# Window attention and a Fourier layer on one Trainium2 core: transposing q and k on VectorE in 32-element blocks

## The chip, the cores and the metric

The kernel runs on one core of one Trainium2 chip. The metric is the device time of an execution in microseconds, the median over runs. TensorE (PE; PEld is its weight load), VectorE (DVE), ScalarE (ACT) and GpSimd (POOL) each work through a queue of their own, in order, and wait for each other through semaphores. SyncE (SP) issues the transfers.

## The reference

Two layers are applied to x of shape (8, 192, 64, 64), all in fp32. A token is a pixel with its 192 channels.

```python
# layer 0: attention in windows of 8 x 8 tokens, 6 heads of 32, then an MLP
shortcut = layer_norm(tokens(x), norm1_g, norm1_b)
q, k, v = windows(shortcut) @ qkv_w.T + qkv_b            # 64 tokens a window
attn = einsum('bhnd,bhmd->bhnm', l2n(q), l2n(k)) * temperature
kth = top_k(attn, 16)[..., -1:]
attn = where(attn >= kth, attn, -100.0)
attn = softmax(attn + rpb, axis=-1)
out = einsum('bhnm,bhmd->bhnd', attn, v) @ proj_w.T + proj_b
x2 = shortcut + out
x2 = x2 + gelu(layer_norm(x2) @ fc1_w.T + fc1_b) @ fc2_w.T + fc2_b
# layer 1: a pointwise network on the 2-D spectrum, then an MLP
xf = fft2(layer_norm(x2), norm='ortho')
h = gelu([xf.real, xf.imag] @ fc1_w.T + fc1_b) @ fc2_w.T + fc2_b     # 2 -> 16 -> 2
x3 = x2 + ifft2(h, norm='ortho').real
out = x3 + gelu(layer_norm(x3) @ mlp1_w.T + mlp1_b) @ mlp2_w.T + mlp2_b
```

## The kernel before

An image of 64 x 64 pixels is cut into eight bands of 512 tokens (eight windows). A band is done in the generators `front` (load, transpose to tokens, layer norm, back to channels, q, k and v, their norms), `attention` (once for each half band `hb`, four windows and six heads) and `back` (projection, MLP of layer 0). Layer 1 of an image follows in twelve groups of 16 channels, `forward`, `pointwise`, `inverse` (the transforms as products with cosine and sine matrices, and the network between them), and in eight bands of `leave` (MLP and store). `mlp` is shared by `back` and `leave`: for each of three pairs of 128 hidden units the products L587 (channels 0 to 127) and L600 (the other 64, in 64-row tiles), Gelu (L571), and at the end L630.

q, k and v of a band: `part_a` multiplies the first 128 channels of the normalized tokens `xn` by the weights, q and k into `pq` (L744) and v into `pv` (L745), with the same 128 tokens as stationary operand; `part_b` does the same for the other 64 channels in two 64-row tiles (L758) and adds the bias of q and k (L761). The index p is one half of the tokens each time, and a row of `pq` is a token. The results are copied to `qk` and `vv` through the helper `copy` (L786), squared and summed for the norms (L708 or L710, L712), and the norms' inverse roots are taken on GpSimd.

The attention of a half band: q and k are scaled by their norms (L798); eight TensorE transposes of 96 x 128 turn them to channels (L804) into one PSUM tile `qt`, which ScalarE or VectorE copies to `qkt` (L786); 24 products of 64 x 64 (four windows, six heads) give the scores (L821), three row groups of 32 channels each; the scores are copied to `s`, the 16 largest of a row are found on VectorE by max, match_replace and max for each of twelve groups (L844 to L846), the others masked (L849, L851), and the softmax follows on GpSimd, ScalarE and VectorE (L854 to L864). TensorE transposes the weights (L871) and multiplies with v (L896).

Nothing runs in the order of the source. Each generator yields operations `op(engine, weight, mode, get, put, after, done)`, and `issue` plays them as a list scheduler while the program is built: it keeps a clock for each engine, takes among the operations that can start soon the one with the earliest begin plus urgency, where the urgency is 300 times the due time of its task (`at_band`, `at_group` and the lists in `streams`), and lets an operation of engine `EITHER` go to ScalarE or VectorE, whichever would end first. `get` and `put` count the buffers: four PSUM tiles `ps` of two banks each, one `qkt`, one `qk`, one `xn`, five `att`, seven `h`. `mode` is the shape of TensorE's tiles; a change of it is priced at 20 units. What comes out is one fixed order for each engine; the waits at run time are those of the semaphores.

Of the kernel before, what the change touches and what calls it, by code (L numbers as in the profile page):

```python
# [8 lines left out]
FP = mybir.dt.float32  # L9
# [6 lines left out]
C = 192  # L16
CA = 128
HC = 96
HW = 64
BAND = 512  # L20
HALF = 256
ROW = 768
# [6 lines left out]
def op(engine, weight, mode=None, get="", put="", after=None, done=None, put_too=""):  # L29
    return engine, weight, mode, get.split(), (put + " " + put_too).split(), after, done  # L30


def issue(streams, units):
# [26 lines left out]
    def start(queue):  # L60
        if queue[0]:
            gen, place = queue[0].pop(0)
            task = {"gen": gen, "queue": queue, "urgency": 300 * place, "last": (None, 0)}
            queue[1] += 1
            task["order"] = (queue[1], len(live), place)
            live.append(task)
            advance(task, None)

    for tasks, width in streams:
        queue = [list(tasks), 0]  # L70
        for _ in range(width):
            start(queue)
    while live:
        best, ready = {}, {}
        for task in live:
            engines, weights, kind, get, put, after, done = task["op"]
# [8 lines left out]
            for name in set(get):  # L85
                n = get.count(name)
# [19 lines left out]
        for engine, found in ready.items():  # L106
            first = min(begin + cost for _, begin, cost, *_ in found) + 15
# [14 lines left out]
        engine, begin, change_cost, task, weight = choice  # L122
        _, _, kind, get, put, after, done = task["op"]
# [15 lines left out]
def kernel(  # L139
# [18 lines left out]
    nc = tc.nc  # L158
    B = x.shape[0]
    NB = HW * HW // BAND  # L160
# [7 lines left out]
    def psum(name):  # L168
        return psp.tile([128, 2, 512], FP, tag="ps", name=name)
# [381 lines left out]
    def mlp(src, nm, w1, fc1_bias, w2, then=None):  # L551
# [12 lines left out]
        copy(done, hn, pc[:, :ROW])  # L564
        hs = []

        def gelu(fp, ph):
            yield op("act", 138, "gelu", put="ps", done=("gelu", nm, fp))
            h = sb.tile([128, 2, BAND], FP, tag="h", name=f"h_{nm}_{fp}", bufs=H_BUFS)
            for k in range(2):  # L570
                nc.scalar.activation(  # L571
                    h[:, k].rearrange("p (t n) -> p t n", t=2),
                    ph[:, :, k * HALF : (k + 1) * HALF],
                    AF.Gelu,
                    bias=fc1_bias[:, 2 * fp + k : 2 * fp + k + 1],
                )
            hs.append(h)

        for fp in range(3):
# [30 lines left out]
            for n, (weight, kind, product) in enumerate(halves[::-1] if fp == 1 else halves):  # L610
                get = ("ps h h h" if fp == 0 else "ps") if n == 0 else ""
                after = None if fp == 0 and n == 0 else []
                yield op(
                    "pe", weight, kind, get=get, put="hn" if fp == 2 and n == 1 else "", after=after
                )
                if n == 0:
                    ph = psum(f"mh_{nm}_{fp}")
                product(n == 0)
            yield from gelu(fp, ph)
        last = [("gelu", nm, fp) for fp in range(3)]  # L620
        for half in range(2):
            if half == 0:
# [20 lines left out]
    def front(b, i):  # L643
# [91 lines left out]
        def values(whole):  # L735
            done = yield op(EITHER, (80, 96), put="ps", after=[whole], done=("vv", b, i))
            copy(done, vv.rearrange("p t a c -> p t (a c)"), pv[:, :, : 2 * C])

        for p in range(2):
            def part_a(first):  # L740
                for t in range(2):
                    tok = xn[:, (2 * t + p) * 128 : (2 * t + p + 1) * 128]
                    flags = dict(start=first, stop=not first, skip_group_check=True)
                    nc.tensor.matmul(pq[:, t, : 2 * C], tok, wqkv[0][:, : 2 * C], **flags)  # L744
                    nc.tensor.matmul(  # L745
                        pv[:, t, p * C : (p + 1) * C], tok, wqkv[0][:, 2 * C :], **flags
                    )

            def part_b(first):
                flags = dict(skip_group_check=True, stop=not first)  # L750
                for to, cols in (
                    (pq[:, :, : 2 * C], slice(0, 2 * C)),
                    (pv[:, :, p * C : (p + 1) * C], slice(2 * C, 3 * C)),
                ):
                    for t in range(2):
                        rows = slice(64 * t, 64 * t + 64)
                        tok = xn[rows, BAND + p * 128 : BAND + (p + 1) * 128]
                        nc.tensor.matmul(to[:, t], tok, wqkv[1][rows, cols], start=first, **flags)  # L758
                for t in range(2):
                    rows = slice(64 * t, 64 * t + 64)  # L760
                    nc.tensor.matmul(  # L761
                        pq[:, t, : 2 * C], ones3[rows], qb3[rows], start=False, **flags
                    )

            if p == 0:
                yield op("pe", 192, "full", get=f"ps ps {places[0]} {places[1]}", after=[normal, "qkv"])
                pq, pv = psum(f"pq_{nm}_{p}"), psum(f"pv_{nm}")
                part_a(True)
                yield op("pe", 112, "row64")
                part_b(False)  # L770
            else:
                yield op("pe", 112, "row64", get="ps", after=[])
                pq = psum(f"pq_{nm}_{p}")
                part_b(True)
                whole = yield op("pe", 192, "full", put="xn")
                part_a(False)
            yield squares(p, pq)
        yield values(whole)

        yield op("pool", 368, after=[normal, "rows"], done=("xt", b, i))  # L780
# [3 lines left out]
    def copy(done, to, of):  # L784

        (nc.scalar.copy if done[0] == "act" else nc.vector.tensor_copy)(to, of)  # L786
# [3 lines left out]
    def attention(b, i, hb):  # L790
# [5 lines left out]
        nf = nrm.rearrange("p a h -> p (a h)")  # L796
        scale = nc.gpsimd if scaled[0] == "pool" else nc.vector
        scale.tensor_tensor(qk3, qk3, nf.unsqueeze(2).to_broadcast([128, 24, 32]), ALU.mult)  # L798
        yield op("pe", 87, "full", get="ps qkt", put=held[b, i][0] if hb == 1 else "")
        pt = psum(f"qt_{nm}")  # L800
        for j in range(2):
            for c in range(2):
                for p in range(2):
                    nc.tensor.transpose(  # L804
                        pt[:HC, j, c * 256 + p * 128 : c * 256 + (p + 1) * 128],
                        qk[:, p, j * C + c * HC : j * C + (c + 1) * HC],
                        ident,
                    )
        done = yield op(EITHER, (100, 121), put="ps")
        qkt = sb.tile([HC, 2, 2, 256], FP, tag="qkt", name=f"qkt_{nm}", bufs=1)  # L810
        copy(done, qkt.rearrange("p j c t -> p j (c t)"), pt[:HC])

        yield op("pe", 58, "s", get="ps ps att", put="qkt")
        ps01, ps2 = psum(f"s_{nm}_0"), psum(f"s_{nm}_1")
        pss = [ps01[:, 0], ps01[:, 1], ps2[:, 0]]
        for wi in range(4):
            for c in range(2):
                for h3 in range(3):
                    rows = slice(32 * h3, 32 * h3 + 32)
                    tok = slice(wi * 64, wi * 64 + 64)  # L820
                    nc.tensor.matmul(  # L821
                        pss[h3][64 * c : 64 * c + 64, tok],
                        qkt[rows, 0, c, tok],
                        qkt[rows, 1, c, tok],
                        start=True,
                        stop=True,
                    )
        done = yield op(EITHER, (59, 69), put="ps")
        s = sb.tile([128, 3, 4, 64], FP, tag="att", name=f"s_{nm}", bufs=ATT_BUFS)
        copy(done, s[:, 0:2].rearrange("p h w k -> p h (w k)"), ps01[:, :, :256])  # L830
        done = yield op(EITHER, (39, 43), put="ps")
        copy(done, s[:, 2].rearrange("p w k -> p (w k)"), ps2[:, 0, :256])

        shape = [128, 3, 4, 64]
        row = lambda t: t.unsqueeze(3).to_broadcast(shape)
# [145 lines left out]
    def forward(b, n):  # L981
# [36 lines left out]
        for j in range(2):  # L1018
            for e in range(2):
                for c in range(4):  # L1020
# [142 lines left out]
    def leave(b, j):  # L1163
# [40 lines left out]
    bands = [(b, i) for b in range(B) for i in range(NB)]  # L1204
    at_band = lambda b, i, late: b + i / NB + late
    groups = [(b, n) for b in range(B) for n in range(NG)]
    at_group = lambda b, n: b + 1.17 + .685 * n / NG
    layer1 = (vec(N2G), vec(N2B))
    streams = [
        ([(setup_qkv(), -1)], 1),  # L1210
# [2 lines left out]
        ([(setup_mlp(0, lambda: (wfc1, wfc2), vec(G2), vec(B2), ["rows", (None, 3000)]), -0.5)], 1),  # L1213
        ([(setup_layer1(), 0.2)], 1),
        ([(setup_mlp(1, lambda: wmlp, *layer1, ["layer1", ("att", 0, 5, 1)]), 0.2)], 1),
        ([(front(b, i), at_band(b, i, -.135)) for b, i in bands], 2),
        ([(attention(b, i, hb), at_band(b, i, .015)) for b, i in bands for hb in range(2)], 4),
        ([(back(b, i), at_band(b, i, .28)) for b, i in bands], 2),
        ([(forward(b, n), at_group(b, n)) for b, n in groups], 1),
        ([(pointwise(b, n, k), at_group(b, n)) for b, n in groups for k in range(2)], 2),  # L1220
        ([(inverse(b, n), at_group(b, n)) for b, n in groups], 1),
        ([(leave(b, j), b + 1.81 + .435 * j / NB) for b, j in bands], 2),
    ]
    with tc.manual_schedule():
        issue(streams, units)
# [80 lines left out]
```

## Time and profile before

| | |
|---|---|
| median of 3 runs | 4932.9 us (4930.42 to 4936.1) |
| profiled execution, its own time | 4943.11 us |
| its span | 4941.3 us |
| granted TensorE clock, mean | 0.977 |
| TensorE busy | 4702.8 us |
| VectorE busy | 2797.7 us |
| ScalarE busy | 2744.7 us |
| GpSimd busy | 2381.0 us |
| HBM read and written | 29.29 and 25.17 MB |

The times of the parts come from the one profiled execution; the span reaches from its first instruction to its last. A line such as "L804 PE MATMUL qt<-ident,qk ... x1024 | 151.7, 297 | 60.7 <-..." is a group of instructions: line, engine, operation, tile written and tiles read, count, busy time in us, mean duration in ns, and the idle time of the engine just before them with what ended it. An fp32 product appears as two records, a transpose as one. TensorE's records overlap each other, so that the mean duration is longer than the distance from one start to the next, and the busy times of groups that follow each other share some time. The slices at the top of the prediction are 40 equal parts of the span in tenths.

### The profile page before, as it was taken

How to read it: one execution, taken by the hardware profiler on the slowest of the kernel's cores; microseconds unless marked ns; L12 is line 12 of the kernel's file. 1: busy time of each engine (PE TensorE's matmuls, PEld its weight loads, DVE VectorE, ACT ScalarE, POOL GpSimd, SP SyncE). 2: the span in 40 equal slices, each digit the busy share in tenths (PEclk: the TensorE clock that was granted, in tenths of full speed). 3: DMA queues.
4: the chain of work that ended last, by engine and by line, in shares of the span. 5: the costliest groups of instructions: out<-in, count | busy, mean ns of one | idle time of the engine just before them, and what ended most of it. 6: DMA issues, size and time to landing. Idle time of an engine off the chain costs nothing.

```text
span 4941.3 us, 147257 instructions
## 1 busy us (share of the span) xinstructions
PE 4702.8 (95%) x63818; PEld 3780.0 (76%) x63818; DVE 2797.7 (57%) x10326; ACT 2744.7 (56%) x3866; POOL 2381.0 (48%) x2208
## 2 busy tenths in 40 slices
PE   6888999999999999999999999999999999999989
PEld 4667777886778877888678877788777887778768
DVE  6778566456665466655665556645666546562112
ACT  3555666446655566555755566645666456653553
POOL 5677555346554455454653555545555445541100
PEclk7898999999999999999999999999999999999999
DMA  2000000000000000000000000000000000000000
GB/s 55 11 8 11 9 9 5 23 14 9 9 12 17 18 6 9 13 19 15 9 5 14 22 14 6 9 14 24 9 6 9 20 18 9 2 2 20 9 2 26
DMA packets 54112, 64.09 MB, mean 13 GB/s; under 512 B 17583, under 2 KB 36218, under 8 KB 53466
## 3 DMA queue, kind: packets, MB, share of 16 engines
q1 hardware_dynamic: 53454, 54.68, 3.8%
q8 instruction: 502, 8.22, 0.7%
q14 instruction: 144, 1.18, 0.1%
q10 hardware_dynamic: 12, 0.00, 0.0%
HBM read 29.29 MB, written 25.17 MB: 11 GB/s over the span
## 4 chain that ended last, share of the span: by engine, by line
PE 85%; ACT 5%; DVE 5%; POOL 3%; issue 2%; DMA 0%; SPq 0%; ACTq 0%; DVEq 0%; POOLq 0%
PE mo_d L630 10%; PE mo_b L630 9%; PE fh L1067 8%; PE mh_d L587 7%; PE fo L1094 7%; PE mh_b L587 7%; PE mh_d L600 4%; PE mh_b L600 4%; PE pq L744 3%; ACT fh L1050 3%; PE qt L804 2%; PE fa L997 2%; PE at L871 2%; PE fb L1115 2%; PE fy L1142 2%
## 5 line engine op out<-in xcount | busy, mean ns | idle before, releaser
L1050 ACT ACTIVATE fh<-fh,ab 128x1024 f32<-128x1024 f32 x768 | 815.1, 1112 | 163.9 <-PE fh L1067 160.2
L854 POOL TENSOR_TENSOR s<-s,top 128x768 f32<-128x768 f32 x128 | 193.8, 1514 | 917.5 <-DVE s L851 870.8
L730 POOL TENSOR_TENSOR nrm<-nrm,mhalf 128x24 f32<-128x24 f32 x128 | 551.9, 4311 | 10.7
L630 PE MATMUL mo_b<-wfc,h_b 128*128 128x192 f32 x3072 | 518.0, 327 | 0.0
L630 PE MATMUL mo_d<-wmlp,h_d 128*128 128x192 f32 x3072 | 512.3, 327 | 0.0
L630 PEld LDWEIGHTS mo_b<-wfc,h_b 128*128 128x128 f32 x3072 | 499.2, 190 | 10.3 <-issue 5.8
L630 PEld LDWEIGHTS mo_d<-wmlp,h_d 128*128 128x128 f32 x3072 | 498.6, 190 | 7.2 <-issue 4.6
L1067 PE MATMUL fh<-fz,w1p 32*128 32x248 f32 (+1 forms) x6144 | 467.6, 404 | 30.1 <-ACT fh L1050 23.3
L571 ACT ACTIVATE h_d<-mh_d,fcb 128x512 f32<-128x512 f32 x384 | 242.1, 684 | 436.0 <-PE mh_d L600 278.1
L1067 PEld LDWEIGHTS fh<-fz,w1p 32*128 32x128 f32 x6144 | 293.0, 185 | 149.5 <-issue 67.3
L844 DVE MAX8 top<-s 128x8 f32<-128x64 f32 x1536 | 320.9, 209 | 129.0 <-ACT s L786 127.9
L1094 PE MATMUL fo<-fh,w2p 128*32 128x264 f32 (+1 forms) x6144 | 387.2, 389 | 3.9 <-ACT fh L1050 2.3
L846 DVE MAX8 top<-s 128x8 f32<-128x64 f32 x1536 | 349.9, 228 | 53.4
L587 PE MATMUL mh_b<-hn_b,wfc_a 128*128 128x256 f32 x1536 | 377.0, 389 | 3.2 <-ACT hn_b L786 1.9
L587 PE MATMUL mh_d<-hn_d,wmlp_a 128*128 128x256 f32 x1536 | 370.7, 386 | 0.8 <-ACT hn_d L786 0.8
L864 POOL TENSOR_TENSOR s<-s,rsum 128x768 f32<-128x768 f32 x128 | 191.2, 1494 | 300.4 <-DVE top L844 144.5
L587 PEld LDWEIGHTS mh_b<-hn_b,wfc_a 128*128 128x128 f32 x1536 | 280.0, 191 | 67.7 <-issue 26.5
L587 PEld LDWEIGHTS mh_d<-hn_d,wmlp_a 128*128 128x128 f32 x1536 | 280.6, 190 | 55.3 <-issue 18.1
L845 DVE MATCH_REPLACE8 s<-top,s 128x64 f32<-128x64 f32 x1536 | 320.3, 209 | 0.1
L1094 PEld LDWEIGHTS fo<-fh,w2p 128*32 128x32 f32 x6144 | 185.6, 111 | 152.8 <-issue 33.4
L571 ACT ACTIVATE h_b<-mh_b,fcb 128x512 f32<-128x512 f32 x384 | 243.1, 686 | 97.3 <-PE mh_b L600 50.6
L1180 DVE TENSOR_TENSOR zt<-mo_d,xy 128x768 f32<-128x768 f32 x64 | 61.3, 957 | 377.2 <-PE mo_d L630 345.5
(220 smaller groups left out, 9311.2 us busy)
## 6 DMA issues: line engine op xcount, KB each, us to landing
xin<-in_x SPq DMA_DIRECT2D x64, 256.0 KB
out<-z SPq DMA_DIRECT2D x64, 256.0 KB
xin<-in_x SPq DMA_DIRECT2D x128, 64.0 KB
out<-z SPq DMA_DIRECT2D x128, 64.0 KB
wfc<-in_wfc SPq DMA_DIRECT2D x1, 576.0 KB
wmlp<-in_wmlp SPq DMA_DIRECT2D x1, 576.0 KB
wfc_a<-in_wfc SPq DMA_DIRECT2D x1, 384.0 KB
wfc_b<-in_wfc SPq DMA_DIRECT2D x2, 192.0 KB
```

The lines of the kernel that those rows point to most:

```text
L571: nc.scalar.activation(h[:, k].rearrange("p (t n) -> p t n", t=2), ph[:, :, k * HALF : (k + 1) * HALF], AF.Gelu, bias=fc1_bias[:, 2 * fp + ...
L587: nc.tensor.matmul(ph[:, t, k * HALF : (k + 1) * HALF], w1[0][:, f], hn[:, t * HALF : (t + 1) * HALF], start=(first and k == 0), stop=not ...
L600: nc.tensor.matmul(ph[:, t, k * HALF : (k + 1) * HALF], w1[1][rows, f], hn[rows, BAND:ROW], start=(first and k == 0), stop=not first, skip ...
L630: nc.tensor.matmul(acc[:, j, t * C : (t + 1) * C], hs[f // 2][:, f % 2, q * 128 : (q + 1) * 128], w2[:, f, ORDER[t]], start=(f == 0 and t ...
L730: nc.gpsimd.tensor_tensor(nf, nf, mhalf[:, :24], ALU.pow)
L844: nc.vector.max(first, of)
L845: nc.vector.match_replace(s2, first, of, -3.0e38)
L846: nc.vector.max(top[:, k // 4, k % 4, 8:16], s2)
L854: nc.gpsimd.tensor_tensor(s, s, top[:, :, :, 0:1].to_broadcast(shape), ALU.subtract)
L1050: nc.scalar.activation(hs[hf, k], ph, AF.Gelu, bias=ab[:, 0:1])
L1067: nc.tensor.matmul(phs[k // 2][:, k % 2, cols], w1p[i][rows, hf].rearrange("p h v -> p (h v)"), fz[rows, :] if rhs is None else zu[rows, : ...
L1094: nc.tensor.matmul(po[rows, :] if i == 0 else pou[rows, :, 1 : U - 1], w2p[i][:, hf].rearrange("p a v -> p (a v)"), hs[hf, k // 2][:, k % ...
```

## The change

q and k are turned by one VectorE instruction per half band in place of eight TensorE transposes and a copy. It transposes blocks of 32 x 32: 32 tokens of one parity of one window against the 32 channels of one head. For that the products of q and k take their tokens with a stride of two (`by_block`), so that half p holds the tokens of parity p, and the 32 partitions of a quadrant hold one window's; the blocks of the two parities are written interleaved, which restores the order of tokens in `qkt`. The scores then lie in four row groups, one for each window, and in two PSUM tiles with two windows each. v keeps dense tokens and gets products of its own after those of q and k.

Beside it, the planner is given other numbers: urgency 360 in place of 300 per unit of due time, other due times, the Gelu of a pair of hidden units yielded after the products of the next pair, and the two copies of `fz` as two operations. The prices of TensorE's new operations and of the transpose are in the diff.

```diff
-            task = {"gen": gen, "queue": queue, "urgency": 300 * place, "last": (None, 0)}
+            task = {"gen": gen, "queue": queue, "urgency": 360 * place, "last": (None, 0)}
...
-        def gelu(fp, ph):
-            yield op("act", 138, "gelu", put="ps", done=("gelu", nm, fp))
+        def gelu(fp, ph, last):
+            yield op("act", 138, "gelu", put="ps", after=[last], done=("gelu", nm, fp))
...
-            yield from gelu(fp, ph)
+            if fp > 0:
+                yield from gelu(fp - 1, *held_)
+            held_ = ph, last
+        yield from gelu(2, *held_)
...
+        def by_block(half, p):
+            return half.rearrange("c (n b) -> c b n", b=2)[:, p]
+
+        def qk_a(pq, p, first):
+            for t in range(2):
+                tok = by_block(xn[:, t * HALF : (t + 1) * HALF], p)
+                nc.tensor.matmul(
+                    pq[:, t, : 2 * C], tok, wqkv[0][:, : 2 * C],
+                    start=first, stop=not first, skip_group_check=True,
+                )
...
+        yield op("pe", 128, "full", get=f"ps {places[0]} {places[1]}", after=[normal, "qkv"])
+        pq = psum(f"pq_{nm}_0")
+        qk_a(pq, 0, True)
+        last = yield op("pe", 80, "row64")
+        qk_b(pq, 0, False)
+        yield squares(0, pq)
+        yield op("pe", 80, "row64", get="ps", after=[])
+        pq = psum(f"pq_{nm}_1")
+        qk_b(pq, 1, True)
+        yield op("pe", 128, "full")
+        qk_a(pq, 1, False)
+        yield squares(1, pq)
+        yield op("pe", 128, "full", get="ps", after=[])
+        pv = psum(f"pv_{nm}")
...
+        whole = yield op("pe", 64, "row64", put="xn")
...
-        yield op("pe", 87, "full", get="ps qkt", put=held[b, i][0] if hb == 1 else "")
-        pt = psum(f"qt_{nm}")
...
-                    nc.tensor.transpose(
-                        pt[:HC, j, c * 256 + p * 128 : c * 256 + (p + 1) * 128],
-                        qk[:, p, j * C + c * HC : j * C + (c + 1) * HC],
-                        ident,
-                    )
-        done = yield op(EITHER, (100, 121), put="ps")
-        qkt = sb.tile([HC, 2, 2, 256], FP, tag="qkt", name=f"qkt_{nm}", bufs=1)
-        copy(done, qkt.rearrange("p j c t -> p j (c t)"), pt[:HC])
+        yield op("dve", 90, get="qkt", put=held[b, i][0] if hb == 1 else "")
+        qkt = sb.tile([128, 12, 64], FP, tag="qkt", name=f"qkt_{nm}", bufs=1)
+        nc.vector.transpose(
+            qkt.rearrange("p h (k a) -> p a h k", a=2), qk.rearrange("p a (h d) -> p a h d", d=32)
+        )
...
-        yield op("pe", 58, "s", get="ps ps att", put="qkt")
+        yield op("pe", 55, "s", get="ps ps att", put="qkt")
+        pss = [psum(f"s_{nm}_{k}") for k in range(2)]
+        for h3 in range(3):
+            for c in range(2):
+                for wi in range(4):
+                    rows = slice(32 * wi, 32 * wi + 32)
                     nc.tensor.matmul(
+                        pss[wi // 2][64 * c : 64 * c + 64, wi % 2, h3 * 64 : (h3 + 1) * 64],
+                        qkt[rows, 3 * c + h3],
+                        qkt[rows, 6 + 3 * c + h3],
...
-        yield op("dve", 118, put="ps ps", done=("fz", b, n))
         for k in range(2):
+            yield op("dve", 43 + 33 * k, put="ps", done=("fz", b, n) if k else None)
...
-    at_group = lambda b, n: b + 1.17 + .685 * n / NG
+    at_group = lambda b, n: b + 1.055 + .755 * n / NG
...
-        ([(front(b, i), at_band(b, i, -.135)) for b, i in bands], 2),
-        ([(attention(b, i, hb), at_band(b, i, .015)) for b, i in bands for hb in range(2)], 4),
-        ([(back(b, i), at_band(b, i, .28)) for b, i in bands], 2),
+        ([(front(b, i), at_band(b, i, -.12)) for b, i in bands], 2),
+        ([(attention(b, i, hb), at_band(b, i, -.07)) for b, i in bands for hb in range(2)], 4),
+        ([(back(b, i), at_band(b, i, .2)) for b, i in bands], 2),
...
-        ([(leave(b, j), b + 1.81 + .435 * j / NB) for b, j in bands], 2),
+        ([(leave(b, j), b + 1.69 + .55 * j / NB) for b, j in bands], 2),
```

More of the change, by code (lines that the diff above doesn't have):

```diff
@@ L612, in mlp @@
                 after = None if fp == 0 and n == 0 else []
-                yield op(
+                last = yield op(
                     "pe", weight, kind, get=get, put="hn" if fp == 2 and n == 1 else "", after=after
@@ L737, in values @@
             copy(done, vv.rearrange("p t a c -> p t (a c)"), pv[:, :, : 2 * C])
-        for p in range(2):
[L740 to L746, printed above, removed]
-                    )
[L749 to L777, printed above, removed]
@@ new lines, in by_block @@
+        def by_block(half, p):
[4 more added lines that the diff above has]
+                nc.tensor.matmul(
+                    pq[:, t, : 2 * C],
+                    tok,
+                    wqkv[0][:, : 2 * C],
+                    start=first,
+                    stop=not first,
+                    skip_group_check=True,
+                )
@@ new lines, in qk_b @@
+        def qk_b(pq, p, first):
+            flags = dict(skip_group_check=True, stop=not first)
+            for t in range(2):
+                rows = slice(64 * t, 64 * t + 64)
+                tok = by_block(xn[rows, BAND:ROW], p)
+                nc.tensor.matmul(
+                    pq[:, t, : 2 * C], tok, wqkv[1][rows, : 2 * C], start=first, **flags
+                )
+            for t in range(2):
+                rows = slice(64 * t, 64 * t + 64)
+                nc.tensor.matmul(pq[:, t, : 2 * C], ones3[rows], qb3[rows], start=False, **flags)
@@ new lines, in front @@
+        pv = psum(f"pv_{nm}")
+        for p in range(2):
+            for t in range(2):
+                nc.tensor.matmul(
+                    pv[:, t, p * C : (p + 1) * C],
+                    xn[:, (2 * t + p) * 128 : (2 * t + p + 1) * 128],
+                    wqkv[0][:, 2 * C :],
+                    start=(p == 0),
+                    stop=False,
+                    skip_group_check=True,
+                )
+        whole = yield op("pe", 64, "row64", put="xn")
+        for p in range(2):
+            for t in range(2):
+                rows = slice(64 * t, 64 * t + 64)
+                nc.tensor.matmul(
+                    pv[:, t, p * C : (p + 1) * C],
+                    xn[rows, BAND + p * 128 : BAND + (p + 1) * 128],
+                    wqkv[1][rows, 2 * C :],
+                    start=False,
+                    stop=True,
+                    skip_group_check=True,
+                )
@@ L798, in attention @@
         scale.tensor_tensor(qk3, qk3, nf.unsqueeze(2).to_broadcast([128, 24, 32]), ALU.mult)
-        yield op("pe", 87, "full", get="ps qkt", put=held[b, i][0] if hb == 1 else "")
-        pt = psum(f"qt_{nm}")
-        for j in range(2):
-            for c in range(2):
-                for p in range(2):
-                    nc.tensor.transpose(
-                        pt[:HC, j, c * 256 + p * 128 : c * 256 + (p + 1) * 128],
-                        qk[:, p, j * C + c * HC : j * C + (c + 1) * HC],
-                        ident,
-                    )
-        done = yield op(EITHER, (100, 121), put="ps")
-        qkt = sb.tile([HC, 2, 2, 256], FP, tag="qkt", name=f"qkt_{nm}", bufs=1)
-        copy(done, qkt.rearrange("p j c t -> p j (c t)"), pt[:HC])
-        yield op("pe", 58, "s", get="ps ps att", put="qkt")
[L814 to L820, printed above, removed]
+        yield op("dve", 90, get="qkt", put=held[b, i][0] if hb == 1 else "")
+        qkt = sb.tile([128, 12, 64], FP, tag="qkt", name=f"qkt_{nm}", bufs=1)
+        nc.vector.transpose(
+            qkt.rearrange("p h (k a) -> p a h k", a=2), qk.rearrange("p a (h d) -> p a h d", d=32)
+        )
+        yield op("pe", 55, "s", get="ps ps att", put="qkt")
+        pss = [psum(f"s_{nm}_{k}") for k in range(2)]
+        for h3 in range(3):
+            for c in range(2):
+                for wi in range(4):
+                    rows = slice(32 * wi, 32 * wi + 32)
                     nc.tensor.matmul(
-                        pss[h3][64 * c : 64 * c + 64, tok],
-                        qkt[rows, 0, c, tok],
-                        qkt[rows, 1, c, tok],
+                        pss[wi // 2][64 * c : 64 * c + 64, wi % 2, h3 * 64 : (h3 + 1) * 64],
+                        qkt[rows, 3 * c + h3],
+                        qkt[rows, 6 + 3 * c + h3],
                         start=True,
@@ L827, in attention @@
                     )
-        done = yield op(EITHER, (59, 69), put="ps")
         s = sb.tile([128, 3, 4, 64], FP, tag="att", name=f"s_{nm}", bufs=ATT_BUFS)
-        copy(done, s[:, 0:2].rearrange("p h w k -> p h (w k)"), ps01[:, :, :256])
-        done = yield op(EITHER, (39, 43), put="ps")
-        copy(done, s[:, 2].rearrange("p w k -> p (w k)"), ps2[:, 0, :256])
+        for k in range(2):
+            done = yield op(EITHER, (49, 56), put="ps")
+            copy(
+                done,
+                s[:, :, 2 * k : 2 * k + 2].rearrange("p h w k -> p w h k"),
+                pss[k][:, :, :C].rearrange("p w (h k) -> p w h k", h=3),
+            )
         shape = [128, 3, 4, 64]
```

## The prediction

> **What bounds the kernel now.** I read the busy table and the slices first, then the chain, then the stretches, and only then the groups of the lines that change.
>
> ```profile
> PE 4702.8 (95%) x63818; PEld 3780.0 (76%) x63818; DVE 2797.7 (57%) x10326; ACT 2744.7 (56%) x3866; POOL 2381.0 (48%) x2208
> ...
> PE   6888999999999999999999999999999999999989
> ...
> PE 85%; ACT 5%; DVE 5%; POOL 3%; issue 2%; DMA 0%; SPq 0%; ACTq 0%; DVEq 0%; POOLq 0%
> ```
>
> TensorE is busy for 95% of the span, every other engine for less than 60%, and the chain that ended last runs on TensorE for 85% of the way. A busy TensorE can still be a waiting one, so the stretches matter more (columns: length, then busy time of PE, PEld, DVE, ACT, POOL):
>
> ```profile
> 800.00:1600.00 800.00, 779.18 (x10158) 633.33 (x10157) 470.22 (x1736) 451.17 (x640) 383.58 (x371) 0.99 0.05 13
> 1600.00:2400.00 800.00, 777.58 (x10814) 625.32 (x10812) 464.84 (x1709) 463.21 (x648) 412.61 (x376) 1.00 0.04 13
> 2400.00:3200.00 800.00, 776.40 (x11366) 617.80 (x11368) 479.35 (x1755) 472.54 (x646) 403.85 (x368) 0.99 0.04 11
> ```
>
> In the steady part TensorE has 21 to 24 us of idle in 800, some 3%. So a microsecond of TensorE work taken out there is nearly a microsecond of the span. The idle that is left is 4941.3 - 4702.8 = 238.5 us, of which about 85 lie in the first 400 us (TensorE busy 66.7, 69.3 and 178.8 us in 100, 100 and 200). What ends it is in the waits (who waited for whom, us, times, longest):
>
> ```profile
> PE qt L804 <- DVE qk L798: 28.0, 5, 12.1
> PE fh L1067 <- ACT fh L1050: 23.3, 26, 1.6
> PE qt L804 <- POOL qk L798: 21.2, 3, 14.0
> PE fz L1022 <- ACT fh L1050: 19.0, 24, 1.9
> PE s L821 <- ACT qkt L786: 14.4, 13, 2.4
> ```
>
> Two kinds: TensorE at the transposes of q and k, waiting for their scaling (few and long, nearly all in the first 400 us), and TensorE waiting for ScalarE's Gelu to give a PSUM slot back (many, short).
>
> The groups that change, and a stretch of TensorE's timeline (start, length of the merged group):
>
> ```profile
> L804 PE MATMUL qt<-ident,qk 128*96 128x128 f32 x1024 | 151.7, 297 | 60.7 <-DVE qk L798 28.0 <-POOL qk L798 21.2 <-ACT fh L1050 8.7
> L786 ACT COPY qkt<-qt 96x1024 f32<-96x1024 f32 x106 | 106.8, 1007 | 115.3 <-PE qt L804 114.8
> L786 DVE COPY qkt<-qt 96x1024 f32<-96x1024 f32 x22 | 26.4, 1199 | 28.0 <-PE qt L804 27.6
> L712 DVE TENSOR_REDUCE nrm<-sq 128x24 f32<-128x768 f32 x128 | 121.1, 946 | 173.4 <-ACT sq L708 143.3 <-POOL sq L710 29.0
> ```
> ```profile
> 2002.10 1.08 PE L804 MATMUL qt<-ident,qk 128*96 128x128 f32 x8
> 2003.02 0.33 PE L924 MATMUL pp<-wprojr,ot 128*128 128x192 f32 x1
> ...
> 2015.78 0.91 PE L744 MATMUL pq<-wqkv_a,xn 128*128 128x384 f32 x2
> 2016.53 0.49 PE L745 MATMUL pv<-wqkv_a,xn 128*128 128x192 f32 x2
> 2016.85 0.81 PE L744 MATMUL pq<-wqkv_a,xn 128*128 128x384 f32 x2
> 2017.50 0.49 PE L745 MATMUL pv<-wqkv_a,xn 128*128 128x192 f32 x2
> ```
>
> Neighbouring groups overlap, so the group's 151.7 us is not what the span gives back. What it gives back is start to start: 2003.02 - 2002.10 = 0.92 us for the eight transposes of one half band.
>
> [...] No run here shows that instruction; the nearest row that reads 768 elements, L712, takes 946 ns. [...] the first pair of L744, straight after 32-row tiles, takes 0.75 us start to start, the second 0.65, so 0.10 us at the entry. [...] no run here shows a strided weight load.
>
> **The change, part by part.**
>
> *Transposes off TensorE.* 64 bands x 2 halves = 128 times 0.92 us = 117.8 us less of TensorE. Bounds: 8 x 0.109 us (the spacing inside a group) x 128 = 112 below, the group's 151.7 above. I take 117.8, all on the path, for 97% of the steady stretch is TensorE's.
>
> *Evacuation of the transposes gone.* ScalarE loses 106.8 us, VectorE 26.4. Both had cover, so nothing directly; PSUM loses one tenant per half band.
>
> *Transposes on VectorE.* 128 times 0.95 us [...] = 121 us. With 26.4 gone and, by the order of the new program, fewer copies and normalizations there (98 tensor_scalar of about 0.45 us go to ScalarE), VectorE rises by about 50 to 95 us, to at most 2893 of some 4810 us, 60%. The cover is its 40% of idle, so zero; without cover it is 121 us. The wait it adds: the transpose stands in VectorE's queue behind whatever series of maxima or statistics is ahead, after the scaling and after the last scores that read `qkt` (one buffer). Behind it on VectorE wait the next half band's maxima. TensorE's s matmuls wait for it, and all that stands behind them in TensorE's queue. The old chain, 0.92 us transposes and a 1.0 us copy, is replaced by one step of 0.95, so the path from scaling to scores is 1 us shorter. Bounds: 10 us better (the startup waits at qt, 49 us, lose part) to 0.5 us worse at each of 128 (64 us). I take 0: the startup waits turn up at s.
>
> *Scores.* The same 24 products per half band, now in four row groups in place of three. The group's busy time, 108.6 us, is 0.85 us per half band. If the pace is that of the row groups it falls by a quarter (27 us), if it is that of issuing, by nothing. I take 8. Evacuation: 512 and 256 elements (585 and 381 ns on ScalarE) become twice 384, the same sum.
>
> *v by its own products.* Same columns, same number of loads and matmuls, no DMA in the step; the products of v stand after both of q and k, so `pv` holds its PSUM slot for less time, and `xn` is released by the last v product rather than the last q product. What is added is changes of tile shape: counted along the instruction order, 2178 before and 2215 after, 37 more over the whole program, at 0.1 to 0.2 us: plus 4 to 7, I take 6. The stationary operand of q and k becomes every second token. A weight load of 128 columns takes 190 ns here (L587, L630), one of 32 columns 111 (L1094), so 0.82 ns per column and 85 fixed. At half rate it would be some 295 ns, still under the 323 ns that one of the two records of a 384-column product streams: free. At a quarter, 505 ns, 0.18 us x 768 (512 records of the full part, 256 pairs of the 64-row part) = 140 us. I take 0.
>
> *Planner edits together* (Gelu listed one product later, the two copies of `fz` as two steps, due times, 360 for 300): no instruction more or less beyond the counts above, the SP queue has the same transfers in a slightly changed order, and the transfers are hidden (DMA 0% of the chain). They act on the waits alone. TensorE's waits that end with L1050's Gelu sum to about 78 us (fh 23.3, fz 19.0, lc 10.6, lt 9.0, qt 8.7, the rest small); a lighter ScalarE and an earlier free PSUM slot can take at most that, and a Gelu that comes later while two slots are held can add as much. I take 10 off, with 40 either way.
>
> *Sum.* -118 - 8 + 6 - 10 = -130 us on a span of 4941.3: 4811; the profiled execution was 4943.1, of which 1.8 lies outside the span, so 4813. The median of the runs, 4932.9, is 10.2 below the profiled one; carried over, 4803, which I round to **4800 us**, 2.7% faster. TensorE should be busy for about 4580, and the rest idle as now.
>
> **The rivals.**
>
> *A wait takes the transposes' place (4865).* TensorE runs its queue in order, and the scores now hang on VectorE, whose queue is also in order and full of maxima of 0.2 us in series. If TensorE stands 0.5 us at each of 128 score groups, 64 us come back. For it: before, the copy could go to either of two engines. Against it: the chain is shorter, VectorE is 43% idle, and the steady waits at qt and s are a few us.
>
> *The transposes are slow (4955, slower).* Place: the first score product of each half band. Price: the blocks are written with a stride of two elements, across 32 lanes; [...] It decides from 133 us, that is where each transpose costs TensorE more than 1.0 us of waiting. For it: no row here shows the instruction. [...]
>
> *The strided weight loads show (4940, no change).* At a quarter of the rate, 140 us as above. For it: all weight loads before are dense. Against it: half rate is still hidden.
>
> *The planner's new order does better than I reckon (4725).* The whole 78 us of PSUM waits go.
>
> **How the numbers follow.** Forecast 4740 to 4850: 0.64. The wait, 4850 to 4923: 0.18. Slow transposes: 0.10. Strided loads: 0.04. Below 4740: 0.04. Within 0.2% is 4923 to 4943, about what a measurement of this kernel can tell from no change. Faster: 0.64 + 0.18 + 0.04 = 0.86; same 0.03 and slower 0.10 + 0.01 = 0.11, the strided loads divided between them. The range is 4740 to 4915: it holds the forecast and nearly all of the wait, 0.81.
>
> **What would show it.** Right: PE busy near 4580 with its idle still near 240; the StreamTranspose row on VectorE near 0.95 us x128; s entries in TensorE's waits that sum to less than 60 us; weight loads of the q and k products near 190 ns; L744's successor at 0.65 us per pair. Wrong: [...] weight loads above 323 ns, TensorE's idle up by more than 60 us, or a TensorE busy time that has not fallen by 110 to 130.

## The result, and the profile after

The changed kernel takes 4902.5 us (median, 4900.31 to 4905.3) against 4934.0 in the same comparison: 0.9929 of the time before, with a 95% interval of 0.9915 to 0.9943. That is 31.5 us less by the medians and 35 by the ratio, 0.7%; 2.7% were forecast. Gains and costs below are differences of ratios times 4934 us. The busy table, the slices of TensorE and the chain on the page of the kernel after:

```profile
PE 4604.9 (94%) x62794; PEld 3656.9 (75%) x62794; DVE 2855.5 (58%) x10312; ACT 2681.7 (55%) x3887; POOL 2366.7 (48%) x2195
...
PE   6778999999999999999999999999999999999989
...
PE 75%; POOL 10%; DVE 7%; ACT 5%; issue 2%; DMA 0%; SPq 0%; ACTq 0%; POOLq 0%; DVEq 0%
```

TensorE lost 97.9 us of busy time (4702.8 to 4604.9), but the span fell by only 42.3, from 4941.3 to 4899.0: its idle rose from 238.5 to 294.1, by 55.6 us. The chain says it too: 75% of it on TensorE in place of 85%, and GpSimd at 10% in place of 3%. The same stretches of the steady part as before (length, then busy time of PE, PEld, DVE, ACT, POOL):

```profile
800.00:1600.00 800.00, 775.53 (x9974) 626.72 (x9973) 463.64 (x1666) 441.12 (x652) 390.12 (x370) 0.99 0.05 13
1600.00:2400.00 800.00, 769.78 (x10789) 609.69 (x10795) 487.09 (x1749) 454.69 (x657) 400.68 (x365) 0.99 0.05 13
2400.00:3200.00 800.00, 770.41 (x11385) 605.89 (x11379) 495.25 (x1780) 464.82 (x668) 413.36 (x383) 0.99 0.04 11
```

TensorE idles 24 to 30 us in 800 where it idled 21 to 24. The waits of TensorE after (for whom, us, times, longest):

```profile
PE at L894 <- POOL s L887: 92.7, 23, 14.8
PE s L841 <- DVE qkt L831: 31.6, 15, 9.1
...
PE fh L1090 <- ACT fh L1073: 9.6, 25, 1.3
PE fz L1045 <- ACT fh L1073: 8.1, 18, 0.5
```

The startup waits at the transposes of q and k (28.0 and 21.2 us) are gone, the waits for Gelu (fh, fz) fell, and the scores wait 31.6 us. But the transposes of the softmax (`at`), which had waited 13.6 us for GpSimd's last step, now wait 92.7, in few and long pieces. The line of before:

```profile
PE at L871 <- POOL s L864: 13.6, 10, 5.3
```

The same view for the first 500 us alone, after:

```profile
PE at L894 <- POOL s L887: 68.5, 7, 14.8
PE s L841 <- DVE qkt L831: 27.8, 11, 9.1
```

and before:

```profile
PE qt L804 <- DVE qk L798: 27.4, 4, 12.1
PE qt L804 <- POOL qk L798: 21.2, 3, 14.0
PE s L821 <- ACT qkt L786: 13.0, 11, 2.4
PE at L871 <- POOL s L864: 12.0, 7, 5.3
```

So most of the new wait lies in the first image, where no other layer's work is at hand. It stands there in place of the waits at the transposes of q and k; whether it is the removed work that had covered it is tested below. At the end of the first image (its last `back` in the trace) the kernel after is 17 us late, 481 us in place of 464. The groups that changed, and two weight loads with the stride:

```profile
L831 DVE STREAM_TRANSPOSE qkt<-qk 128x768 f32<-128x768 f32 x128 | 125.1, 977 | 81.4 <-PE s L841 57.1 <-issue 15.0 <-POOL qk L826 4.8
...
L841 PE MATMUL s<-qkt 32*64 32x64 f32 x6144 | 106.3, 240 | 41.3 <-DVE qkt L831 31.6 <-issue 5.6 <-ACT fh L1073 3.3
...
L749 PEld LDWEIGHTS pq<-wqkv_a,xn 128*128 128x128 f32 x512 | 93.5, 200 | 70.3 <-issue 28.6 <-ACT fh L1073 5.5 <-DVE s L868 0.7
...
L763 PEld LDWEIGHTS pq<-wqkv_b,xn 64*128 64x128 f32 x512 | 44.7, 195 | 35.9 <-issue 28.5 <-ACT fh L1073 1.8 <-ACT s L881 1.1
```

The transpose takes 977 ns, and the loads of every second token 200 and 195 ns (193 and 187 dense before). Neither is where the gain went.

### The profile page after: what moved, and what is told of

Same layout as the page of the kernel before. It is cut to its first block, busy times and chain, and to the rows that moved or that the text cites. A ratio compares the mean times of both kernels' runs of the same rounds, so it can differ in the third digit from the quotient of the medians.

```text
span 4899.0 us, 145236 instructions
## 1 busy us (share of the span) xinstructions
PE 4604.9 (94%) x62794; PEld 3656.9 (75%) x62794; DVE 2855.5 (58%) x10312; ACT 2681.7 (55%) x3887; POOL 2366.7 (48%) x2195
## 4 chain that ended last, share of the span: by engine, by line
PE 75%; POOL 10%; DVE 7%; ACT 5%; issue 2%; DMA 0%; SPq 0%; ACTq 0%; POOLq 0%; DVEq 0%
PE mo_d L633 10%; PE mo_b L633 9%; PE fh L1090 7%; PE mh_d L587 6%; PE mh_b L587 6%; PE fo L1117 6%; POOL nrm L733 4%; PE mh_d L600 3%; PE mh_b L600 3%; PE pq L749 3%; ACT fh L1073 2%; PE fa L1020 2%; PE fy L1165 2%; PE fb L1138 2%; PE pq L763 2%
## 5 line engine op out<-in xcount | busy, mean ns | idle before, releaser
L867 DVE MAX8 top<-s 128x8 f32<-128x64 f32 x1536 | 319.9, 208 | 38.9 <-ACT s L814 38.6
```

The source lines that it names most:

```text
L867: nc.vector.max(first, of)
```

## The experiments

The theories at the outset: *cover* (Q in the expectations: TensorE's work was not all on the path; what was removed had covered other engines' delays, and returns as idle); *plan* (P: a microsecond of TensorE is worth a microsecond, but the planner's new numbers took the gain back; S is a special case, a later end of the first image); *terms* (the new operations cost TensorE or VectorE more than reckoned: stride, v's own products, the transpose). R came later: any other order of the same work moves the time. The results first; busy and idle are TensorE's in the profiled span, "first" is its idle in the first 500 us. "Core" is the change of products and transpose with before's planner (urgency, due times, Gelu order, one step for `fz`).

| run | ratio to before (95%) | busy | idle | first |
|---|---|---|---|---|
| before | 1 | 4702.8 | 238.5 | 95.7 |
| after | 0.9929 (0.9915-0.9943) | 4604.9 | 294.1 | 121.3 |
| e2, core | 0.9898 (0.9876-0.9921) | 4603.9 | 283.0 | 121.5 |
| e3, before with all planner edits | 1.0128 (1.0108-1.0148) | 4708.5 | 286.4 | 116.9 |
| e4, after, dense tokens | 0.9925 (0.9905-0.9945) | 4606.8 | 291.9 | 125.3 |
| e6, after, each transpose twice | 0.9987 (0.9980-0.9994) | 4607.7 | 320.7 | 136.1 |
| e7, after, old Gelu order | 0.9912 (0.9899-0.9926) | 4608.9 | 286.1 | 130.0 |
| e9, after, old due times in the first image | 0.9972 (0.9962-0.9983) | 4606.8 | 320.9 | 139.3 |
| e12, core with `fz` in two steps | 0.9840 (0.9826-0.9853) | 4576.2 | 275.7 | 123.2 |
| e13, before with `fz` in two steps | 1.0003 (0.9997-1.0010) | 4692.1 | 238.5 | 95.6 |
| e14, before, urgency 310 | 1.0014 (1.0006-1.0022) | 4670.5 | 262.1 | 97.2 |
| e15, e12 with urgency 310 | 0.9892 (0.9877-0.9906) | 4588.6 | 294.6 | 121.9 |
| e16, e12 with urgency 290 | 0.9976 (0.9967-0.9984) | 4622.0 | 301.0 | 122.3 |
| e17, e12, v's products beside q and k | 0.9997 (0.9988-1.0006) | 4613.7 | 319.1 | 147.8 |
| e19, e12 with urgency 360 | 0.9972 (0.9963-0.9980) | 4602.6 | 314.0 | 137.8 |
| e20, e12 with the new due times | 0.9947 (0.9933-0.9962) | 4606.5 | 301.9 | 123.3 |
| e21, after, urgency 300 | 0.9924 (0.9905-0.9943) | 4606.6 | 289.4 | 121.5 |
| e23, before, more TensorE work | 1.0134 (1.0118-1.0151) | 4801.4 | 198.2 | 83.1 |
| e5, after, TensorE work put back | 1.0083 (1.0062-1.0103) | 4716.7 | 259.0 | 116.0 |
| e24, e12, TensorE work put back | 1.0002 (0.9996-1.0009) | 4705.3 | 236.8 | 104.0 |

### The two halves

e2 is the kernel after with the planner's numbers, the order of Gelu and the step of `fz` as before; e3 is the kernel before with all of these as after.

```diff
-            task = {"gen": gen, "queue": queue, "urgency": 360 * place, "last": (None, 0)}
+            task = {"gen": gen, "queue": queue, "urgency": 300 * place, "last": (None, 0)}
...
-    at_group = lambda b, n: b + 1.055 + .755 * n / NG
+    at_group = lambda b, n: b + 1.17 + .685 * n / NG
...
-        ([(attention(b, i, hb), at_band(b, i, -.07)) for b, i in bands for hb in range(2)], 4),
+        ([(attention(b, i, hb), at_band(b, i, .015)) for b, i in bands for hb in range(2)], 4),
```

> The new products and the VectorE transpose with the planner's numbers, the Gelu order and the fz copies of the kernel before. Theory P (a microsecond of TensorE work is worth a microsecond, and the planner edits made TensorE wait where it did not): about 4820 us. Rival Q (waits come in the place of the removed work whatever the planner's numbers are): about 4900 us, as the changed kernel.

> The kernel before with all planner edits (urgency, due times, Gelu order, fz copies) and TensorE's transposes kept. P: slower than before by what the changed kernel is short of, 60 to 100 us, about 5010 us. Q: within 20 us of before, 4915 to 4955 us.

The core alone gives 50 us, nearer to Q; the plan alone costs the kernel before 63, as P said. They don't add up: after is 35 us faster, not 13 slower. The core without the plan has the same TensorE busy time as after to 1 us, and its idle is already 44.5 us above before. So in this order most of the lost gain is lost without any planner edit. In e3, where the transposes are still on TensorE, the softmax's transposes already wait as long as in after:

```profile
PE at L874 <- POOL s L867: 99.4, 37, 11.2
```

### The terms one by one

e4 takes dense tokens for q and k again, so that they belong to other tokens than in the reference; all else is as after.

```diff
-            return half.rearrange("c (n b) -> c b n", b=2)[:, p]
+            return half[:, p * 128 : (p + 1) * 128]
```

> The changed kernel, in its own order, with the tokens of the q and k products taken densely in place of every second one (q and k then belong to other tokens than the scores take them for). If the strided weight loads are free: 4902 us within 5. If they cost 30 to 60 ns for each of 768 loads or pairs: 4860 to 4880 us.

0.9925 against 0.9929: the stride is worth 2 us, within the intervals nothing.

e6 issues each VectorE transpose a second time.

```diff
         nc.vector.transpose(
             qkt.rearrange("p h (k a) -> p a h k", a=2), qk.rearrange("p a (h d) -> p a h d", d=32)
         )
+        nc.vector.transpose(
+            qkt.rearrange("p h (k a) -> p a h k", a=2), qk.rearrange("p a (h d) -> p a h d", d=32)
+        )
```

> The changed kernel, in its own order, with each VectorE transpose issued twice, 125 us more of VectorE work. If VectorE's time at the transpose is covered as forecast: within 15 us of 4902. If the scores wait for the transpose all along (the rival of the forecast): plus 60 to 125 us, 4960 to 5030 us.

VectorE is busy for 117 us more (2972.7 against 2855.5), and that costs 29 us, a quarter; the expectation had at most 15 or at least 60. The waits of TensorE in this run show them:

```profile
PE at L897 <- POOL s L890: 90.9, 25, 14.8
PE s L844 <- DVE qkt L834: 53.6, 25, 10.1
```

The wait at the scores rose from 31.6 to 53.6, the one at the softmax's transposes did not. So VectorE's transpose is mostly covered, and its own share of the lost gain, if the second one is a measure of the first, is near 30 us.

e7 puts the Gelu of a pair straight after its products again.

```diff
-            if fp > 0:
-                yield from gelu(fp - 1, *held_)
-            held_ = ph, last
-        yield from gelu(2, *held_)
+            yield from gelu(fp, ph)
```

> The changed kernel with the Gelu listed straight after its own products as before, the other planner edits kept. If the later Gelu costs (two PSUM slots held): about 4885 us. If it helps: about 4920 us. S says that it matters little beside the due times: within 10 us of 4902.

8 us less than after, with overlapping intervals: not told apart.

### S, the first image

```diff
-        ([(attention(b, i, hb), at_band(b, i, -.07)) for b, i in bands for hb in range(2)], 4),
+        ([(attention(b, i, hb), at_band(b, i, -.07 if b else .015)) for b, i in bands for hb in range(2)], 4),
```

and likewise for `front` and `back`.

> The changed kernel with the due times of before for front, attention and back of the first image alone. Theory S (the shortfall lies in the first image, where TensorE waits for the softmax and the removed work gives nothing, and the new due times make that worse; from the second image on the reckoned gain arrives): the first image ends some 20 us earlier and the time is about 4880 us. Theory Q (the waits are spread over all images): within 5 us of 4902.

It went the other way: the kernel is 21 us slower than after, against both theories, and the first image ends at 489 us, not earlier than 481. (Of the end alone 8 us say little: e4, in the order of after, has it at 488.) S as "the new due times make the first image late" fell.

### `fz`, and orders next to each other

e12 is e2 with one edit more, the two copies of `fz` as two operations; e13 makes that edit in the kernel before.

```diff
-        yield op("dve", 118, put="ps ps", done=("fz", b, n))
         for k in range(2):
+            yield op("dve", 43 + 33 * k, put="ps", done=("fz", b, n) if k else None)
```

> The core alone (4884 us) with the two fz copies as two operations, which give back PSUM earlier. If PSUM slots bind TensorE in the steady part: 4870 to 4880 us. If not: 4884 within 8 us, which is the spread that another order of the plan gives.

> The kernel before with the two fz copies as two operations and nothing else. If the earlier PSUM slot is worth something by itself, as its gain of 25 us on the core alone suggests: 15 to 30 us faster than before. If that gain was the luck of an order (R): between 15 us faster and 30 us slower, and no rule.

e12 gains 29 us on e2 and is the fastest version found: 4859.5 us, 0.9840, faster than both kernels. On the kernel before the same edit is worth 0.0003. That raises the doubt whether it is the edit or the order that happened to come out. So the urgency was moved by a thirtieth, which changes only what the planner makes of the same work: its order, and which of ScalarE and VectorE takes an operation of engine `EITHER`:

```diff
-            task = {"gen": gen, "queue": queue, "urgency": 300 * place, "last": (None, 0)}
+            task = {"gen": gen, "queue": queue, "urgency": 310 * place, "last": (None, 0)}
```

> The kernel before with urgency 310 in place of 300 and nothing else: another order of the same work. Theory R (every other order of the plan moves the time by some 10 to 30 us, mostly up from a tuned one, so that part of what the planner edits did is the order and not their purpose): 4940 to 4970 us. If orders close to each other run alike: within 8 us of before.

> The core with the fz copies, ratio 0.984, with urgency 310 in place of 300. R: 10 to 30 us slower than with 300, ratio 0.986 to 0.990. If not: 0.984 within 0.0015.

> The core with the fz copies with urgency 290: another order of the same work. From its neighbours at 300 and 310 the ratio is 0.984 to 0.991; outside of that, one order says little about an edit.

The kernel before moves by 0.14%. e12 moves by 0.5% with 310 and by 1.4%, 67 us, with 290 in place of 300. So the 29 us can't be credited to the edit of `fz`. Part of the 67 us goes with TensorE's clock (us from first to last instruction, mean granted clock), e12:

```profile
core 0: 4851.9 us, clock 0.978
```

e16:

```profile
core 0: 4922.9 us, clock 0.970
```

(1 - 0.978) x 4851.9 = 107 us of clock not granted against (1 - 0.970) x 4922.9 = 148: the difference is an estimated 41 us, and TensorE's busy time for the same products is 45.8 us longer (4622.0 against 4576.2). The order with more idle (301.0 against 275.7) has the lower clock. That the idle is what lowered it is not shown by these runs. The two orders differ in more than that: e16 gives ScalarE 123 instructions more (3939 against 3816) and 81.1 us more of busy time, among them 18 more loads of its function table (ACT_TABLE_LOAD, 220 against 202, 1.283 us each in the traces of before and after), and TensorE waits longer at `fh` for ScalarE's Gelu, e12 and then e16:

```profile
PE fh L1087 <- ACT fh L1070: 10.2, 26, 1.3
```
```profile
PE fh L1087 <- ACT fh L1070: 36.6, 78, 1.8
```

The first 500 us are alike (idle 123.2 and 122.3). How much of the 67 us each of these carries was not tested; fewer table loads alone don't make a fast order, for e15 has 194.

e19 takes urgency 360 and e20 the new due times, each on e12; e21 takes after with urgency 300. Their edits are lines of the first diff of this section.

> The core with the fz copies (ratios 0.984 and, at urgency 310, 0.989) with urgency 360 and the due times of before. If the urgency is what costs the first image 20 us: first image ends near 480 us and the ratio is 0.991 to 0.995. If not: ends near 456 us, ratio 0.984 to 0.990.

> The core with the fz copies with the new due times and urgency 300. If the due times cost: first image ends near 480 us, ratio 0.991 to 0.995. If not: near 456 us and 0.984 to 0.990.

> The changed kernel with urgency 300 in place of 360 and nothing else. If the urgency is the cause: ratio 0.984 to 0.989. If due times and Gelu order are: 0.991 to 0.996.

On e12 both edits cost (65 and 53 us), on the kernel after the urgency costs nothing (0.9924 and 0.9929). A step from 300 to 290 costs as much (67 us, e16), so these runs single out no edit.

### v beside q and k

e17 takes the products of v back beside those of the first half of q and k, so that they bring no change of tile shape of their own; v then holds a PSUM tile for longer.

```diff
-        yield op("pe", 128, "full", get=f"ps {places[0]} {places[1]}", after=[normal, "qkv"])
-        pq = psum(f"pq_{nm}_0")
+        yield op("pe", 256, "full", get=f"ps ps {places[0]} {places[1]}", after=[normal, "qkv"])
+        pq, pv = psum(f"pq_{nm}_0"), psum(f"pv_{nm}")
```

> The core with the fz copies (ratio 0.984), the products of v put straight after those of q and k of the first half, full part beside full part and 64-row part beside 64-row part, so that v needs no tile shape of its own. If v's own products cost the 20 us that the trace shows in their starts: 10 to 20 us faster, ratio 0.980 to 0.982. If it is lost in the order of the plan: 0.984 within 0.005, either way.

It is 77 us slower than e12. The product of v that stands at the change of shape (its 64-row part), summed from start to start without waits, is 9.3 us above before in e12 and 0.1 here; but the wait for the softmax, 74.7 us in e12, grew. The waits of e17:

```profile
PE at L888 <- POOL s L881: 99.9, 33, 21.3
PE s L835 <- DVE qkt L825: 41.6, 8, 16.6
```

and the first image ends at 509 us. A cheaper term of TensorE's sum is here again not a shorter span.

### What a microsecond of TensorE is worth

The test of the step that failed: each engine keeps its order, and TensorE is given eight transposes of a constant ahead of each score group, written into the PSUM tiles that the scores then overwrite. They wait for nothing new. The edit in the kernel after (e5) and in e12 (e24):

```diff
         pss = [psum(f"s_{nm}_{k}") for k in range(2)]
+        for n in range(8):
+            nc.tensor.transpose(pss[n // 4][:HC, n // 2 % 2, n % 2 * 128 : n % 2 * 128 + 128], ident[:, :HC], ident)
```

and in the kernel before (e23), where they come beside the eight that are there:

```diff
         pss = [ps01[:, 0], ps01[:, 1], ps2[:, 0]]
+        for n in range(8):
+            to = (ps01, ps2)[n // 4]
+            nc.tensor.transpose(to[:HC, n // 2 % 2, n % 2 * 128 : n % 2 * 128 + 128], ident[:, :HC], ident)
```

> The changed kernel, in its own order, with eight TensorE transposes of a constant ahead of each group of score products, about 118 us of TensorE work in all; they leave the result as it is. P: 4902 plus 100 to 130, about 5015 us. Q: 4902 plus 30 to 60, about 4945 us.

> The kernel before, in its own order, with eight more TensorE transposes of a constant ahead of each group of scores, 112 us of TensorE work that leaves the result as it is. If the order of before is bound by TensorE as the forecast read it: plus 100 to 125 us, ratio 1.020 to 1.025. If the worth is that of the changed kernel's order, two thirds: plus 65 to 85 us, ratio 1.013 to 1.017.

> The core with the fz copies (ratio 0.984), in its own order, with eight TensorE transposes of a constant ahead of each group of scores. At two thirds of 112 us: ratio 0.998 to 1.001. At the full time: 1.006 to 1.009.

The work is reckoned at 1024 x 0.109 us = 112 us each time; TensorE's busy time rose by 111.8 in e5, 98.6 in e23 and 129.1 in e24. It costs (1.0083 - 0.9929) x 4934 = 76 us on after, 66 on before and (1.0002 - 0.9840) x 4934 = 80 on e12: 0.68, 0.59 and 0.71 of a microsecond for each, with the intervals 0.5 to 0.8 (e5 lies between its two expectations, e23 and e24 at the two thirds). Put against the busy time that each added, it is 0.62 to 0.68. Stretches of the kernel before (the start and the middle):

```profile
0.00:500.00 500.00, 404.33 (x4644) 326.56 (x4648) 378.57 (x1517) 243.65 (x391) 343.57 (x299) 0.86 0.08 21
500.00:4300.00 3800.00, 3690.76 (x51508) 2961.27 (x51501) 2233.20 (x8181) 2202.07 (x3061) 1910.49 (x1754) 0.99 0.04 12
```

and of e23:

```profile
0.00:500.00 500.00, 416.89 (x4992) 338.92 (x4994) 378.57 (x1521) 248.28 (x397) 348.63 (x302) 0.91 0.08 21
500.00:4300.00 3800.00, 3717.85 (x51162) 2997.89 (x51162) 2194.36 (x8069) 2165.06 (x3011) 1877.84 (x1731) 0.99 0.04 12
```

The added work goes into TensorE's idle in both: 95.7 to 83.1 us in the first 500, 109.2 to 82.1 in the middle. Over the whole span the idle fell by 40.3 us in e23, 35.1 in e5 and 38.9 in e24. A part is clock: the busy time rose least where the granted clock rose (e23, 0.977 to 0.984) and most where it did not (e24, 0.978 to 0.977), with e5 between (0.973 to 0.978). This is *cover*, shown in three orders with the order of every engine held.

Two limits. The added transposes do not stand where the removed ones stood: those came ahead of the copy that the scores wait for, these come behind it, and fill the wait for it too. That wait fell by 11 us in e23 (14.4 to 3.3), 12 in e24 (42.0 to 29.8) and 14 in e5. With these added back, the worth would be an estimated 0.69 to 0.82; the old place was not tried. And the largest new wait, as far as these runs show, is not one that the removed work had covered. The waits of e5:

```profile
PE at L896 <- POOL s L889: 93.3, 23, 14.8
PE s L843 <- DVE qkt L831: 18.1, 7, 8.3
```

With TensorE's work back, the softmax's transposes wait 93.3 us, as in after (92.7); in e24 they wait 66.7 against 74.7 in e12. That wait belongs to the new orders, and e3 has it with the old transposes.

It also divides the result. With TensorE's work put back, e24 has before's time, busy time and idle (1.0002; 4705.3 and 236.8 against 4702.8 and 238.5): in that order the rest of the change costs nothing, and taking 112 us from TensorE gives 80. In the order of after, the rest of the change costs 41 us (1.0083), and taking the 112 away gives 76; 35 remain. So of the 95 us that are missing from the forecast 130, 42 are the worth of the transposes (118 forecast, 76 found) and 53 are the rest (12 better forecast, 41 worse found).

## Why the prediction was wrong

The direction was right, the size was not. Two steps failed.

*The first*, 42 of the missing 95 us, is "a microsecond of TensorE work taken out there is nearly a microsecond of the span", with "all on the path, for 97% of the steady stretch is TensorE's". The 3% of idle was read as a bound on what could be lost. It isn't one: it tells how little idle there is while the work is there, not how much of the work stands in front of someone else's delay. The runs at a fixed order show 0.6 to 0.7. For the 98 us that TensorE lost that is 60 to 70 us, not 98. What returned as idle is, as far as the waits of e5 and after tell, mostly at the scores (31.6 against 18.1) and at Gelu (51 against 42). An eighth of the transposes lies in the first image, where TensorE idles for a fifth of the time (95.7 of 500 us).

*The second*, 53 us, is the sum of all else: -8 + 6 - 10 was forecast, with the planner's edits "on the waits alone" and 40 either way. In the order of after it costs 41. A new order of a planner was taken to be about as good as the old one; the runs of the same operations lie between 0.9840 and 0.9976. Which part of an order costs what is open.

*"TensorE's … idle near 240 as now"* was a term of the sum, -10. Measured: +55.6. Of this, 35 is what e5 takes back; the other 20 go with the order. What the term reckoned with did occur: the waits that end with Gelu fell from 78 us to 51, and the scores wait more, as written (40.9 us, under the 60 named). What it did not reckon with is an order in which GpSimd's softmax is what TensorE finds late, 13.6 to 92.7. The rival "a wait takes the transposes' place" gave 4865, for 64 us at the scores; there the waits rose by 20 (all entries of s, 20.8 to 40.9).

*Transposes off TensorE, -118* was right as work: 97.9 us of busy time less in all, with the next two terms taken out, leaves 118. *v by its own products, +6*: +22 from start to start in the trace after (11.0 us for the first products of q and k, which now follow other tiles, 11.0 for v's 64-row part); the number of tile changes was right to a few (40 more in the records, 37 forecast), its price was not. 0.10 us at the entry was only a part: in the trace after, the last record of L749 is followed by a tile of another shape 416 ns after its start and by one of its own shape after 323, the last of v's 64-row part after 253 and 156, so an estimated 0.09 to 0.10 us at the exit too. *Scores, -8*: 1.6 us less from start to start (101.6 to 100.0), where a pace set by the number of row groups would have given 27; here it did not set the pace. These two make the 22 us by which the busy time, 4604.9, is above the sum's 4583; but 4576.2 (e12) and 4622.0 (e16), for the same operations, show that an order alone moves it as far.

*Right*: the transpose on VectorE (0.95 forecast, 0.977 us measured; L712 before, 0.946, was the nearest row), its cover in the main (of a second one a quarter shows; none was forecast), the free stride (e4, 0.9925 against 0.9929; loads of 200 and 195 ns against 193 and 187), the lighter ScalarE (-63.0 us) and the heavier VectorE (+57.8; 50 to 95 forecast).

No trace of before shows the transpose or a strided load: that the stride would be free, and the 4955 of the rival with slow transposes, were the author's estimates. One sum is off without bearing on this: the rival at 4725 counts the 10 us of the planner's edits twice.

*The planner's edits*, taken together at -10 with 40 either way: they cost 63 us on the kernel before; on the core after stands 15 us behind e2, with intervals that overlap. In ten orders of the new operations (e2, e7, e9, e12, e15, e16, e19, e20, e21, after) the gain was 12 to 79 us, in nine of them less than the 64 that 0.65 x 98 us leads to. So a worth found at a fixed order is no promise for an order made anew.

*What stays open*: what TensorE's work is worth at the place where it was removed; which edit makes after's order 44 us worse than e12's. 25 us of these lie in the first image (481 against 456 us at its end), but no single edit was found that carries them: its end is 480 us with urgency 300 in after, 475 with the old Gelu order, 489 with the old due times, and in e12 463 with the new due times and 500 with urgency 360. A part is granted clock (0.973 in after, 0.978 in e12). That waits of 10 to 15 us in the start depend on which half band's softmax TensorE has next in its queue is argued from the waits and was not tested.

## What to carry to other kernels

Before a removal from the bounding engine is priced at its full time, put a like amount of work in, as near to the same place as can be, with the order of the queues held: here 112 us cost 66, 76 and 80, though TensorE was busy for 97% of the steady part. Ask what each removed piece stood in front of, and above all which stretch (here the first image) isn't bound by that engine. Where a planner writes the order, run neighbouring orders before an edit is credited with a per cent: 290, 300 and 310 of one number gave 0.9976, 0.9840 and 0.9892.

## What was not expected of the hardware

The granted clock of this kernel tends to be lower where TensorE idles more: 0.984 with 198 us of idle (e23), 0.977 with 239 (before), 0.970 with 301 and 321 (e16, e9); but loosely, for e14 has 0.983 with 262 and e20 0.977 with 302. VectorE's transposes of 32-element blocks of fp32, 128 x 768 elements written with a stride of two, take 922 to 1019 ns.
